# Seven block products in place of eight in the input half of two feed-forward blocks

## The chip, the core and the metric

The kernel runs on one core of a Trainium2 chip. A core has engines that work side by side, each through its own queue of instructions in order: TensorE (PE, with the weight loads shown as PEld), VectorE (DVE), ScalarE (ACT), GpSimd (POOL) and SyncE (SP), which here issues all DMAs. On-chip data lies in SBUF; TensorE writes its results to PSUM[...]. The metric is the device time of one execution in microseconds (us), less is better. "Before" is the median of three runs.

## What is computed

A stack of 128 graphs with 128 nodes of 256 features passes through two layers. Layer 0 is a graph-attention (GAT) layer, layer 1 is a relational multi-head attention with 8 heads and 4 relations. Each ends in a feed-forward block 256 -> 1024 -> 256, and these two blocks are what the change is about.

```python
def _L0_gnn_ref(x, adj, W1, a1, W2, a2, w_ff1, b_ff1, w_ff2, b_ff2, ...):
    h = _gat(x, adj, W1, a1, Fout)
    h = _gat(h, adj, W2, a2, W2.shape[1])
    h = _layernorm(x + h, g_ln1, b_ln1)
    ff = jnp.matmul(jax.nn.relu(jnp.matmul(h, w_ff1) + b_ff1), w_ff2) + b_ff2
    return _layernorm(h + ff, g_ln2, b_ln2)

def _L1_gnn_ref(src, adj_matrix, Wq, bq, Wk, bk, Wv, bv, Wo, bo, W1, b1, W2, b2, ...):
    attn = jax.nn.softmax(jnp.einsum('bhid,bhjd->bhij', q, k) / np.sqrt(dh), axis=-1)
    for r in range(4):
        mask = (adj_matrix == r)[:, None]
        out = out + jnp.einsum('bhij,bhjd->bhid', attn * mask, v_r)
    x = _ln(src + out @ Wo + bo, g1, beta1)
    ff = jax.nn.gelu(x @ W1 + b1, approximate=False) @ W2 + b2
    return _ln(x + ff, g2, beta2)
```

All arithmetic is fp32.

## The kernel before

The 128 graphs are taken in 32 groups of four (G = 4), so a group is T = 512 nodes. Each group goes through five stages, which are Python generators: stage_load (L475), stage_gat (L480), stage_ff0 (L487), stage_attention (L490) and stage_ff1 (L498). A generator emits some instructions and yields a number from the table TIMES (L26), its estimate of how long this step lasts. A heap (L511 to L537) always advances the generator whose virtual time is lowest. A stage of group g starts at 100 g plus the stage's offset (L511) minus an entry of EARLY (L35), so some five groups are in flight, and pieces of different stages alternate in each queue. Within the range KEPT (L36) the order of emission on PE and SP is fixed by added dependencies; on ACT, DVE and POOL a scheduler orders the instructions when the program is built.

The feed-forward block, feed_forward (L256), takes the group's features with the feature index on the partitions (hT, from features, L250). The input half runs over four pairs of 128-row slices of the 1024 hidden units. For each slice two matmuls of 512 columns accumulate the two halves of the 256 input features in one PSUM tile (L266), and ACT reads it once, adds the bias and applies ReLU or GELU into an SBUF tile fT (L269). So there are 16 matmuls and 8 activations per block and group. In block terms, with hidden halves, feature halves and node halves, these are eight products of 512 x 128 x 256 and their sums are formed in PSUM by accumulation. The output half (L278) takes the eight fT tiles as stationary operand: 32 matmuls of 256 columns, whose sum DVE adds to the residual (L279).

All PSUM tiles named mm come from one pool of six; one more bank holds adj, the adjacency of the group as fp32 (L361), and one av, the attention output.

The features are turned by transposed (L224): DVE transposes 32 x 32 blocks into a scratch tile z (one buffer), four DMAs write it to DRAM with the blocks in their new places, and one reads it back (L240 to L245). The exponentials of the attention are turned in place in the same way. In the attention, by_relation (L391) makes for each relation r and half of the heads one masked copy of the turned weights eT on DVE (L397), 128 x 512, eight per graph; the product with the values (L416) reads them. values (L399) computes the values of a graph for the four relations (L404), weights (L364) the scores (L371) and their exponentials (L381).

load_group (L89) fetches three inputs of a group at once: xT for the GAT matmuls, the adjacency mask, and x, which is both the residual and the tile tok in which the group's state lives until it is stored. There are two xT buffers, four for the mask, which is held until the attention has copied it, and six for tok. The first two groups are fetched ahead of most weights (L118 to L128 and L155).

Of the kernel before, what the change touches and what calls it, by code (L numbers as in the profile page):

```python
# [22 lines left out]
P = 128  # L23
# [3 lines left out]
    "ff pair": 5, "ff half": 14.5, "row": 14, "gat": 18, "wh": 6,  # L27
    "gat copy": 3, "qk": 5, "scores": 5, "turn0": 10, "turn1": 5,
    "v0": 3, "mask0": 2, "av": 7, "v": 3, "mask": 3,
    "end": 2, "lead ff0": 30, "lead att": 32, "lead ff1": 31, "affine": 6,  # L30
# [4 lines left out]
EARLY = {(1, 1): 70, (1,2): 50, (2,0): 80, (2,1): 90, (2,2): 90}  # L35
KEPT = {mybir.EngineType.PE: (250, 3150), mybir.EngineType.SP: (0, 4000)}  # L36
# [15 lines left out]
def graph_layers(ctx: ExitStack, tc: tile.TileContext, a: dict, out: bass.AP):  # L52
# [21 lines left out]
    TB, KB = 5, 6  # L74
# [14 lines left out]
    def load_group(g):  # L89
        xt = ld.tile([P, DC, T], F32, name="xt")  # L90
        nc.sync.dma_start(xt, xT[g])
        at = ld.tile([P, G, N], I32, name="at", bufs=4)
        nc.sync.dma_start(at, adjT[g])
        xg = wk.tile([P, G, D], F32, name="tok", bufs=KB)
        nc.sync.dma_start(xg, x[g])
        return xg, xt, at
# [20 lines left out]
    w2T = wload("W2T", wk.tile([P, DC, D], F32, name="w2T", tag="fT", bufs=FC))  # L117
    first_xt = ld.tile([P, DC, T], F32, name="xt")  # L118
    nc.sync.dma_start(first_xt, xT[0])
    w1T = wload("W1T", wk.tile([P, DC, D], F32, name="w1T", tag="fT", bufs=FC))  # L120
    first_at = ld.tile([P, G, N], I32, name="at", bufs=4)
    nc.sync.dma_start(first_at, adjT[0])
    second_xt = ld.tile([P, DC, T], F32, name="xt")
    nc.sync.dma_start(second_xt, xT[1])
    second_at = ld.tile([P, G, N], I32, name="at", bufs=4)
    nc.sync.dma_start(second_at, adjT[1])
    first_x = wk.tile([P, G, D], F32, name="tok", bufs=KB)
    nc.sync.dma_start(first_x, x[0])  # L128
# [26 lines left out]
    second_x = wk.tile([P, G, D], F32, name="tok", bufs=KB)  # L155
    nc.sync.dma_start(second_x, x[1])
# [31 lines left out]

    folded(wf1, bf1, "01")

# [33 lines left out]
    def transposed(y, t, direct, over=False):  # L224
# [14 lines left out]
        z = y if over else wk.tile([P, n, N], F32, name="z", bufs=1)  # L239
# [10 lines left out]
    def features(y, direct):  # L250

        t = t_tile().rearrange("p (b c n) -> p b c n", b=G, c=DC)
        transposed(y.rearrange("p b (c f) -> p (b c) f", f=P), t.rearrange("p b c n -> p (b c) n"), direct)
        return t

    def feed_forward(y, before, direct, win, bin_, wout, func, by=G):  # L256
# [4 lines left out]
        fT = []  # L261
        for f0 in range(0, FC, 2):
            pair = [ps.tile([P, T], F32, name="mm") for _ in range(2)]
            for c in range(DC):
                for i, p in enumerate(pair):
                    nc.tensor.matmul(p, win[:, c, ts(f0 + i, P)], hT[:, :, c], start=c == 0, stop=c == DC - 1)  # L266
            for i, p in enumerate(pair):
                t = wk.tile([P, T], F32, name="fT", tag="fT", bufs=FC)
                nc.scalar.activation(t, p, func, bias=bin_[:, f0 + i:f0 + i + 1])  # L269
                fT.append(t)  # L270
            yield TIMES["ff pair"]
            if f0 in (2, 4):
                affine(y, before, f0 - 2, 2)
        for b2_ in range(0, G, 2):
            p = ps.tile([P, 2, D], F32, name="mm")
            for b in (b2_, b2_ + 1):
                for f in range(FC):
                    nc.tensor.matmul(p[:, b - b2_], fT[f][:, ts(b, N)], wout[:, f], start=f == 0, stop=f == FC - 1)  # L278
# [33 lines left out]
    def gat_block(direct, tag, xg, xt, at):  # L312
# [17 lines left out]
        yield TIMES["gat copy"]  # L330
        att = yield from gat_weighting(wh, D, cap, direct)
        yield TIMES["gat"]
        y = xg
        for b2_ in range(0, G, 2):
# [3 lines left out]
            nc.vector.tensor_add(y[:, b2_:b2_ + 2], xg[:, b2_:b2_ + 2], p)  # L338
        normalised(y)
        return y, at  # L340

    def attention(y, at, first, direct):

        hT = features(y, first or direct)
        yield TIMES["lead att"]
# [40 lines left out]
        def turned(e):  # L386
            eT = wk.tile([P, H, N], F32, name="eT")
            transposed(e, eT, direct, over=True)
            return eT

        def by_relation(b, eT, ms, parts):  # L391


            ab = adj[:, b][:, None, :].to_broadcast([P, HC, N])
            for r, h in parts:
                m = ms[r, h] = wk.tile([P, HC, N], F32, name="m", bufs=DC * R)
                nc.vector.scalar_tensor_tensor(m, ab, r, eT[:, ts(h, HC)], op0=OP.is_equal, op1=OP.mult)  # L397
# [11 lines left out]
        def weighted(ms, v):  # L409
# [3 lines left out]
            for c in range(DC):  # L413
                for r in reversed(range(R)):
                    for q in reversed(range(HC)):
                        last = nc.tensor.matmul(po[ts(q, DH), c], v[:, r, c * P + q * DH:c * P + (q + 1) * DH],  # L416
                                                ms[r, q // 2][:, c * 2 + q % 2],
# [14 lines left out]
        PARTS = [(r, h) for r in range(R) for h in range(2)]  # L432
        v, ms = values(0), {}
        for k in range(0, 8, 2):
            by_relation(0, eT[0], ms, PARTS[k:k + 2])
            yield TIMES["mask0"]
        for b in range(G):
# [8 lines left out]
            for k in range(0, 8, 2):  # L446
                if b + 1 < G:
                    by_relation(b + 1, eT[b + 1], ms, PARTS[k:k + 2])
# [17 lines left out]
    def ff1(y, direct, by):  # L466
        return feed_forward(y, "11", direct, w1, b1, w2, AF.Gelu, by)
# [3 lines left out]
    x0, x1, x2, masks, loads = {}, {}, {}, {}, {}  # L471
    loads[0] = first_x, first_xt, first_at
    loads[1] = second_x, second_xt, second_at

    def stage_load(g):  # L475
        if g > 1:
# [111 lines left out]
```

## Time and profile before

| | before |
|---|---|
| median of 3 runs | 3284.59 us (3283.44 to 3287.23) |
| the profiled execution | 3284.59 us, span of the core 3282.8 us |
| mean granted TensorE clock | 0.989 |
| DMA traffic | 311.11 MB |

Some rows of the costliest groups (line, engine, operation, output <- input with partitions x elements, count, then busy time and mean ns of one, then the idle time just ahead of them and what ended it):

```profile
L397 DVE SCALAR_TENSOR_TENSOR m<-adj,eT 128x512 f32<-128x512 f32 x1024 | 637.2, 680 | 282.1 <-DMA eT<-zd 252.8
L269 ACT ACTIVATE fT<-mm,col 128x512 f32<-128x512 f32 x512 | 333.0, 696 | 392.7 <-PE mm L266 392.3
L266 PE MATMUL mm<-T,w 128*128 128x512 f32 x1024 | 461.1, 598 | 2.3 <-DVE v L405 1.3
L278 PE MATMUL mm<-w,fT 128*128 128x256 f32 x2048 | 454.5, 379 | 0.0
L278 PEld LDWEIGHTS mm<-w,fT 128*128 128x128 f32 x2048 | 388.4, 190 | 80.3 <-issue 31.0
L279 DVE TENSOR_TENSOR tok<-tok,mm 128x512 f32<-128x512 f32 x128 | 88.0, 687 | 421.3 <-PE mm L278 421.2
```

The mean of one PE matmul is not what it costs in a stream, because consecutive matmuls overlap and the ends are modelled; the busy time of the row already takes overlaps within the row out. Every fp32 matmul stands in the trace as two records: L266 issues 512 matmuls for each of the two blocks and has 1024 records.

### The profile page before, as it was taken

The page shows a single profiled execution, that of the slowest core. Times are in us where ns is not written, and L with a number is a line of the kernel's source. Part 1 is how long each engine was busy: PE and PEld are TensorE (multiplying, and loading weights), DVE is VectorE, ACT ScalarE, POOL GpSimd, SP SyncE. Part 2 cuts the span into 40 slices and gives each one's busy share as a digit, 9 for nine tenths or more (in the row PEclk, how much of TensorE's full clock was granted, in tenths as well). Part 3 has the DMA queues.
Part 4 walks back from the last instruction along what each step waited for, and adds up shares of the span by engine and source line. Part 5 has one row for each costly group of instructions (what it writes and reads, how often), then busy time and mean ns, then how long its engine had stood idle before and what let it go on. Part 6 is the DMA issues. An engine that isn't in the chain of part 4 may idle for free.

```text
span 3282.8 us, 50948 instructions
## 1 busy us (share of the span) xinstructions
PE 3217.6 (98%) x18632; PEld 2086.8 (64%) x18632; DVE 1847.3 (56%) x3765; ACT 1531.9 (47%) x4552; POOL 1206.3 (37%) x1480
## 2 busy tenths in 40 slices
PE   6989999999999999999999999999999999999997
PEld 5656666666666666666666666666666666666655
DVE  2375556565555555555555555565565565565552
ACT  3344445545445545445545445545445545445431
POOL 2224334344234344234344234344234344245321
PEclk8999999999999999999999999999999999999998
DMA  5144445344455344454444455344455344454210
GB/s 171 35 111 81 100 110 113 88 98 89 98 112 111 91 97 89 98 112 109 93 92 94 98 112 109 91 97 91 97 113 109 91 100 88 96 113 91 59 33 13
DMA packets 1146571, 311.11 MB, mean 95 GB/s; under 512 B 898256, under 2 KB 1120976, under 8 KB 1146192
## 3 DMA queue, kind: packets, MB, share of 16 engines
q1 hardware_dynamic: 1146320, 307.85, 42.1%
q8 instruction: 147, 2.41, 0.3%
q14 instruction: 104, 0.85, 0.1%
HBM read 178.67 MB, written 129.10 MB: 94 GB/s over the span
## 4 chain that ended last, share of the span: by engine, by line
PE 94%; DVE 3%; DMA 1%; SPq 1%; ACT 1%; POOL 1%; issue 0%; ACTq 0%; DVEq 0%; POOLq 0%
PE mm L278 26%; PE mm L266 26%; PE mm L404 13%; PE av L416 7%; PE mm L371 4%; PE mm L320 3%; PE mm L350 3%; PE mm L356 3%; PE mm L454 3%; PE mm L328 2%; PE mm L337 2%; DVE m L397 1%; SPq L243 1%; DMA zd<-e 1%; DMA eT<-zd 1%; PE mm L184 0%
## 5 line engine op out<-in xcount | busy, mean ns | idle before, releaser
L383 POOL TENSOR_TENSOR e<-e,s 128x512 f32<-128x512 f32 x256 | 277.8, 1091 | 1576.0 <-DVE s L382 1566.8
L397 DVE SCALAR_TENSOR_TENSOR m<-adj,eT 128x512 f32<-128x512 f32 x1024 | 637.2, 680 | 282.1 <-DMA eT<-zd 252.8
L222 POOL TENSOR_TENSOR tok<-tok,ln_rows 128x512 f32<-128x512 f32 (+1 forms) x636 | 659.0, 1055 | 58.2 <-DVE z L240 19.0
L269 ACT ACTIVATE fT<-mm,col 128x512 f32<-128x512 f32 x512 | 333.0, 696 | 392.7 <-PE mm L266 392.3
L404 PE MATMUL mm<-wv,T 128*128 128x512 f32 x1024 | 469.5, 601 | 0.0
L266 PE MATMUL mm<-T,w 128*128 128x512 f32 x1024 | 461.1, 598 | 2.3 <-DVE v L405 1.3
L266 PE MATMUL mm<-T,wf 128*128 128x512 f32 x1024 | 459.3, 597 | 0.0
L278 PE MATMUL mm<-w,fT 128*128 128x256 f32 x2048 | 454.5, 379 | 0.0
L278 PE MATMUL mm<-wf,fT 128*128 128x256 f32 x2048 | 453.4, 379 | 0.0
L278 PEld LDWEIGHTS mm<-w,fT 128*128 128x128 f32 x2048 | 388.4, 190 | 80.3 <-issue 31.0
L381 ACT ACTIVATE e<-mm,nm 128x128 f32<-128x128 f32 x1024 | 359.3, 386 | 160.8 <-DVE nm L377 149.6
L278 PEld LDWEIGHTS mm<-wf,fT 128*128 128x128 f32 x2048 | 388.8, 190 | 67.3 <-issue 15.7
L216 ACT ACTIVATE tok<-tok,nmr,rstd 128x256 f32<-128x256 f32 x512 | 265.8, 591 | 158.5 <-POOL nmr L214 158.4
L404 PEld LDWEIGHTS mm<-wv,T 128*128 128x128 f32 x1024 | 190.4, 191 | 231.6 <-issue 209.1
L266 PEld LDWEIGHTS mm<-T,wf 128*128 128x128 f32 x1024 | 192.7, 191 | 224.1 <-issue 207.9
L266 PEld LDWEIGHTS mm<-T,w 128*128 128x128 f32 x1024 | 192.0, 191 | 218.6 <-issue 207.3
L279 DVE TENSOR_TENSOR tok<-tok,mm 128x512 f32<-128x512 f32 x128 | 88.0, 687 | 421.3 <-PE mm L278 421.2
L416 PE MATMUL av<-m,v 128*32 128x128 f32 x8192 | 255.7, 275 | 8.6 <-DVE v L405 5.0
L359 ACT ACTIVATE kbd<-mm,col 32x512 f32<-32x512 f32 x256 | 173.9, 679 | 191.5 <-PE mm L356 187.4
L416 PEld LDWEIGHTS av<-m,v 128*32 128x32 f32 x8192 | 217.4, 110 | 56.8 <-issue 45.1
L240 DVE STREAM_TRANSPOSE z<-tok 128x1024 f32<-128x1024 f32 x90 | 111.7, 1241 | 242.3 <-ACT tok L216 220.6
L381 ACT ACTIVATION_READ_ACCUMULATOR e<-mm,nm 128x1 f32 x1024 | 231.5, 226 | 0.0
(87 smaller groups left out, 3178.0 us busy)
## 6 DMA issues: line engine op xcount, KB each, us to landing
zd<-e SPq DMA_DIRECT2D x496, 128.0 KB
eT<-zd SPq DMA_DIRECT2D x124, 512.0 KB
zd<-z SPq DMA_DIRECT2D x360, 128.0 KB
T<-zd SPq DMA_DIRECT2D x90, 512.0 KB
xt<-in_xT_dram SPq DMA_DIRECT2D x32, 512.0 KB
tok<-in_x_dram SPq DMA_DIRECT2D x32, 512.0 KB
out_dram<-tok SPq DMA_DIRECT2D x31, 512.0 KB
e<-zsd SPq DMA_DIRECT2D x60, 256.0 KB
```

What stands on the lines that cost most here:

```text
L216: nc.scalar.activation(y[:, b], y[:, b], AF.Identity, bias=nmr[:, b:b + 1], scale=rstd[:, b:b + 1])
L222: engine.tensor_tensor(y[:, b:b + n], y[:, b:b + n], v[:, None, :].to_broadcast([P, n, D]), op)
L266: nc.tensor.matmul(p, win[:, c, ts(f0 + i, P)], hT[:, :, c], start=c == 0, stop=c == DC - 1)
L269: nc.scalar.activation(t, p, func, bias=bin_[:, f0 + i:f0 + i + 1])
L278: nc.tensor.matmul(p[:, b - b2_], fT[f][:, ts(b, N)], wout[:, f], start=f == 0, stop=f == FC - 1)
L359: nc.scalar.activation(kbd[c][rows, :, q % 2], p[rows], AF.Identity, bias=bk[rows, c:c + 1])
L371: nc.tensor.matmul(scores[h][:, c], qT[rows, c, ts(b, N)], kbd[c][rows, b], start=True, stop=True, tile_position=(h * P // 2, 0))
L381: nc.scalar.activation(eh[:, q], p[:, q], AF.Exp, bias=nm[:, q:q + 1], accum_out=s[:, q:q + 1])
L383: nc.gpsimd.tensor_mul(eh, eh, per_row(s, N))
L397: nc.vector.scalar_tensor_tensor(m, ab, r, eT[:, ts(h, HC)], op0=OP.is_equal, op1=OP.mult)
L404: nc.tensor.matmul(p, hT[:, b, f], wv[:, f, r:r + 2], start=f == 0, stop=f == DC - 1)
L416: last = nc.tensor.matmul(po[ts(q, DH), c], v[:, r, c * P + q * DH:c * P + (q + 1) * DH], ms[r, q // 2][:, c * 2 + q % 2], start=r == R - ...
```

## The change

The input half of both blocks is rewritten in Strassen's form (with Winograd's sums). With the weights in four blocks a (feature half by hidden half) and the features in four blocks b (feature half by node half, two graphs each), four sums of the weight blocks are made once (weight_sums, three new tiles, two blocks overwritten) and four sums of the feature blocks are made on POOL for each block and group (moving_sums). Seven products then give all four blocks of the result. A unit computes two slices of each hidden half; in it each product is two matmuls of 256 columns, one for each slice, which fill one PSUM tile. One tile, chain, takes products 1, 6, 7 and 4 in turn, accumulating, and is read by ACT or DVE between them; a second, side, takes 5 and then 3; a third, p, takes 2. ACT copies partial sums to SBUF, DVE adds others onto them, and ACT applies the function at the end: lo in place in SBUF, one half of hi from the chain. Two units run in alternation.

Beside it: masks are made for all heads of a relation at once, 1024 columns; transposed has no tile z of its own any more, features are turned within their target tile; x is fetched only ahead of the second half of the GAT stage, and the mask is fetched a second time for the attention instead of being held; xT has one buffer, the mask two, tok five; the output half takes the hidden slices in the order in which units finish; TIMES, EARLY, the offsets and KEPT have new numbers, and EARLY now has entries for the last groups too.

```diff
 def load_group(g):
-        xt = ld.tile([P, DC, T], F32, name="xt")
+        xt = ld.tile([P, DC, T], F32, name="xt", bufs=1)
         nc.sync.dma_start(xt, xT[g])
-        at = ld.tile([P, G, N], I32, name="at", bufs=4)
+        return xt, load_mask(g)
+    def load_mask(g):
+        at = ld.tile([P, G, N], I32, name="at")
         nc.sync.dma_start(at, adjT[g])
-        xg = wk.tile([P, G, D], F32, name="tok", bufs=KB)
-        nc.sync.dma_start(xg, x[g])
-        return xg, xt, at
+        return at
...
+    def weight_sums(w, name):
+        half = w.shape[-1] // 2
+        a11, a12, a21, a22 = w[:, 0, :half], w[:, 1, :half], w[:, 0, half:], w[:, 1, half:]
+        s1, s2, s4 = (cst.tile([P, half], F32, name=f"{name}s{i}") for i in (1, 2, 4))
+        nc.vector.tensor_add(s1, a21, a22)
+        nc.vector.tensor_sub(s2, s1, a11)
+        nc.vector.tensor_sub(s4, a12, s2)
+        nc.vector.tensor_sub(a21, a11, a21)
+        nc.vector.tensor_scalar(a22, a22, -1.0, None, op0=OP.mult)
+        return None, a11, a12, s4, a22, s1, s2, a21
...
-        z = y if over else wk.tile([P, n, N], F32, name="z", bufs=1)
         nc.vector.transpose(z, y)
...
+    def moving_sums(hT):
+        b11, b21, b12, b22 = (hT[:, h:h + G // 2, c] for h in (0, G // 2) for c in range(DC))
+        t1, t2, t4 = (wk.tile([P, G // 2, N], F32, name=f"t{i}") for i in (1, 2, 4))
+        nc.gpsimd.tensor_sub(t1, b12, b11)
+        nc.gpsimd.tensor_sub(t2, b22, t1)
+        nc.gpsimd.tensor_sub(b12, b22, b12)
+        nc.gpsimd.tensor_sub(t4, t2, b21)
+        return None, b11, b21, b22, t4, t1, t2, b12
...
-        for f0 in range(0, FC, 2):
-            pair = [ps.tile([P, T], F32, name="mm") for _ in range(2)]
-            for c in range(DC):
-                for i, p in enumerate(pair):
-                    nc.tensor.matmul(p, win[:, c, ts(f0 + i, P)], hT[:, :, c], start=c == 0, stop=c == DC - 1)
-            for i, p in enumerate(pair):
-                t = wk.tile([P, T], F32, name="fT", tag="fT", bufs=FC)
-                nc.scalar.activation(t, p, func, bias=bin_[:, f0 + i:f0 + i + 1])
+        hs = moving_sums(hT)
+        def unit(f0):
+            lo, hi = (wk.tile([P, 2, 2, T // 2], F32, name="fT", bufs=FC // 2) for _ in range(2))
...
+            def product(p, k, first=False):
+                for i in range(2):
+                    nc.tensor.matmul(p[:, i], win[k][:, ts(f0 + i, P)], hs[k], start=first and i == 0, stop=True,
+                                     skip_group_check=True)
+            chain, side = (ps.tile([P, 2, T // 2], F32, name="mm") for _ in range(2))
+            product(chain, 1, True)
+            product(side, 5, True)
+            nc.scalar.copy(lo[:, :, 0], chain)
+            nc.scalar.copy(hi[:, :, 1], side)
+            yield
+            p = ps.tile([P, 2, T // 2], F32, name="mm")
+            product(chain, 6)
+            product(p, 2, True)
+            product(side, 3)
+            nc.scalar.copy(lo[:, :, 1], chain)
+            nc.vector.tensor_add(lo[:, :, 0], lo[:, :, 0], p)
+            nc.vector.tensor_add(lo[:, :, 1], lo[:, :, 1], side)
+            yield
+            product(chain, 7)
+            nc.vector.tensor_add(hi[:, :, 1], hi[:, :, 1], chain)
+            yield
+            product(chain, 4)
+            for i in range(2):
+                nc.scalar.activation(lo[:, i], lo[:, i], func, bias=bin_[:, f0 + i:f0 + i + 1])
+            for i in range(2):
+                f = FC // 2 + f0 + i
+                nc.scalar.activation(hi[:, i, 1], hi[:, i, 1], func, bias=bin_[:, f:f + 1])
+                nc.scalar.activation(hi[:, i, 0], chain[:, i], func, bias=bin_[:, f:f + 1])
+            yield
+        units = [unit(0), unit(2)]
+        for n, now in enumerate(((0,), (1,), (0,), (1,), (0,), (1,), (0,), (1,))):
+            for u in now:
+                next(units[u])
...
         yield TIMES["gat copy"]
+        y = wk.tile([P, G, D], F32, name="tok", bufs=KB)
+        nc.sync.dma_start(y, x[g])
...
-                m = ms[r, h] = wk.tile([P, HC, N], F32, name="m", bufs=DC * R)
-                nc.vector.scalar_tensor_tensor(m, ab, r, eT[:, ts(h, HC)], op0=OP.is_equal, op1=OP.mult)
+                m = ms[r] = wk.tile([P, H, N], F32, name="m", bufs=R)
+                nc.vector.scalar_tensor_tensor(m, ab, r, eT, op0=OP.is_equal, op1=OP.mult)
...
-    stages = (stage_load, -81), (stage_gat, -39), (stage_ff0, 50), (stage_attention, 130), (stage_ff1, 298)
+    stages = (stage_load, -81), (stage_gat, -39), (stage_ff0, 48), (stage_attention, 132), (stage_ff1, 300)
```

In the prediction, L numbers are those of the kernel before; L318, where DVE adds a chain after product 7, is the one of the changed kernel, as are "product", "unit" and "chain".

## The prediction

> **What bounds the kernel now.** I read the page from the top, then the windows by stage, then the timeline of one group. First the busy line, the slices and the chain of waits:
>
> ```profile
> PE 3217.6 (98%) x18632; PEld 2086.8 (64%) x18632; DVE 1847.3 (56%) x3765; ACT 1531.9 (47%) x4552; POOL 1206.3 (37%) x1480
> ...
> PE   6989999999999999999999999999999999999997
> ...
> PEclk8999999999999999999999999999999999999998
> ...
> PE 94%; DVE 3%; DMA 1%; SPq 1%; ACT 1%; POOL 1%; issue 0%; ACTq 0%; DVEq 0%; POOLq 0%
> PE mm L278 26%; PE mm L266 26%; PE mm L404 13%; PE av L416 7%; PE mm L371 4%; PE mm L320 3%; PE mm L350 3%; PE mm L356 3%; PE mm L454 3%; PE mm L328 2%; PE mm L337 2%; DVE m L397 1%; SPq L243 1%; DMA zd<-e 1%; DMA eT<-zd 1%; PE mm L184 0%
> ```
>
> TensorE (PE) is busy nearly throughout, at its full clock, and the chain that ended last is PE work for 94%. L266, the half of feed-forward that the change rewrites, is 26% of it. A busy PE can still have gaps, so the windows (columns: PE, PEld, DVE, ACT, POOL busy, clock, DMA share, GB/s):
>
> ```profile
> 164.00:250.00 86.00, 73.01 (x610) 47.85 (x609) 61.96 (x120) 35.49 (x137) 19.53 (x26) 0.96 0.45 106
> 250.00:1200.00 950.00, 948.70 (x5509) 614.27 (x5508) 551.02 (x1117) 459.52 (x1367) 360.44 (x439) 1.00 0.45 98
> 1200.00:2200.00 1000.00, 1000.00 (x5809) 648.59 (x5808) 584.70 (x1192) 485.98 (x1436) 389.30 (x474) 1.00 0.45 100
> 2200.00:3150.00 950.00, 948.84 (x5558) 611.45 (x5557) 547.29 (x1111) 446.24 (x1318) 358.71 (x439) 1.00 0.43 94
> 3150.00:3200.00 50.00, 43.60 (x324) 27.39 (x323) 31.65 (x66) 24.83 (x87) 21.41 (x24) 0.90 0.14 32
> 3200.00:3283.00 83.00, 64.10 (x336) 41.84 (x334) 19.12 (x47) 16.16 (x28) 15.82 (x24) 0.89 0.04 13
> ```
>
> From 250 to 3150 us PE idles 2.5 us in all; its 65 us of idle time (3282.8 - 3217.6) lie at the two ends. So each microsecond of PE work removed in the middle comes off the time, until something else makes PE wait. What a matmul costs is read from the distance between starts, since PE durations overlap. The timeline (start, length, ...):
>
> ```profile
> 1504.72 7.07 PE L278 MATMUL mm<-wf,fT 128*128 128x256 f32 x32
> 1511.62 1.90 PE L328 MATMUL mm<-wh,e 128*128 128x258 f32 x8
> ...
> 1542.02 3.60 PE L266 MATMUL mm<-T,w 128*128 128x512 f32 x8
> 1545.46 1.89 PE L337 MATMUL mm<-wh,e 128*128 128x256 f32 x8
> ```
>
> Each fp32 matmul leaves two records. Four of 512 columns take 1545.46 - 1542.02 = 3.44 us, 0.860 each; sixteen of 256 columns take 6.90 us, 0.431 each. A matmul of half the width costs half, and each with its own weights.
>
> **What the Trainium skill says.** "TensorE: Matmul & The Clock Gate", Part 2, Step-by-step (what each phase is for): a stream of matmuls is paid by its columns, and the next weights load while the current matmul runs. The trace agrees: weight loads take 190 ns inside records spaced 216 ns. "Perfetto Trace Analysis", Tensor Engine Instruction (MATMUL, LD_WEIGHTS): "ACT/DVE/GPSIMD are strict FIFO"; whatever stands behind a waiting instruction waits too. The trace shows it on DVE: L397 idles 252.8 us in 67 waits for eT. The same page, Optimization Strategy: the same gap repeated for a stretch can mean too few buffers for the next tile. No such gap is in the trace before; the new form, which holds PSUM tiles longer, is where one could arise.
>
> **The change, part by part.**
>
> *Products.* Removed: 2 blocks x 32 groups x 16 matmuls x 0.860 = 880.6 us. Added: 64 x 2 units x 7 products x 2 x 0.431 = 772.4 us. PE gains 108.2 us, 3.38 per group. Each of the 28 needs its own weight load, as L278's do, and those run at 0.431.
>
> *Evictions and sums.* ACT lost 16 activations per group at 333.0/512 = 0.650 us (10.4 us), and gets 12 PSUM copies at 0.59 (L237: 575 and 605 ns), 8 activations of 512 at 0.696 and 16 of 256. The last I price from "ScalarE: Activation LUTs", What ACT_TABLE_LOAD costs (280 ns + 0.833 per element with a bias pointer): 493 ns, an estimate; the same formula gives 707 at 512, where the trace has 696. Sum 20.6, so +10.2 us. DVE gets 12 adds at 0.687 (L279), +8.2. The masks go from 32 at 0.680 to 16 of 1024 columns; L455 (256: 410 ns) and L279 (512: 687) give 1.08 ns a column, so 1.24 us each: 21.8 becomes 19.8, -2.0. POOL gets 8 subtractions of 256 at 0.730 (L222's 256 form), +5.8. Per group, from the middle window (a period is 98.5 us, from L266's start at 1501.29 to 1599.79), ACT goes from 48 to 58 us, DVE from 58 to 64, POOL from 38 to 44, in a new period of at least 95.1. None becomes the bound by its sum; PE's 95 us covers them. If that cover fails, it is by order, not by load.
>
> *Order in the middle.* In the order of instructions of the changed kernel I followed one group by hand, with durations of this trace; 0 is the end of the second score pair. PE then has L343's 16 matmuls (6.9), products 1 and 5 of unit 0, the output projection (0.86), 1 and 5 of unit 1, 6, 2, 3 of each unit, 7 of each, two value tiles (3.44), and product 4 of unit 0, wanted at 21.5. Three waits come close:
> (a) Product 4 accumulates on a PSUM tile that DVE (L318) must first read. On DVE four masks stand ahead, which wait for eT. The first e is transposed at about 6.3 (exponentials 1.5, POOL's scaling with the new subtractions between 5.0, transpose 1.25). The way by DRAM and back then took 9.5 us in one case and 13.8 in another (issue of the first write to the first mask):
>
> ```profile
> 1588.95 2.55 SPq L243 DMA_DIRECT2D zd<-e  x4
> ...
> 1598.42 1.29 DVE L397 SCALAR_TENSOR_TENSOR m<-adj,eT 128x512 f32<-128x512 f32 x2 [1.73 <-DMA eT<-zd]
> ...
> 1524.77 6.41 SPq L243 DMA_DIRECT2D zd<-e  x4
> ...
> 1538.54 2.48 DVE L397 SCALAR_TENSOR_TENSOR m<-adj,eT 128x512 f32<-128x512 f32 x4 [6.40 <-DMA eT<-zd]
> ```
>
> With 9.5: masks 15.8 to 20.7, one add, L318 done at 22.1, PE 0.6 late. (b) The next output half (L343) needs a PSUM tile that ACT's exponentials free, behind two normalisations and twelve activations: ready 29.6, wanted 28.9, 0.7 late. (c) In the second block the GAT product (L403) needs a tile freed by DVE behind three masks: ready 9.3, wanted 8.2, 1.1 late. They sum to 2.4 us per group but do not add: a pause of PE moves what PE wants next and leaves ACT and DVE running. My starting times are good to a microsecond at best, so the bounds are 0 and 2.4 per group; I take 0.6, the first wait alone, on 30 groups: +18 us (0 to 72). Queued behind such a PE wait is all of PE; POOL and ACT wait only for products already issued.
>
> *Transposes, loads, ends.* z becomes the target tile itself, which removes a wait of 21.8 us on DVE that PE never felt: 0. Masks are loaded a second time (32 x 256 KB, 8.4 MB on 311) on DMA engines busy 45%: 0 in the middle, in SP's order ahead of an eT return once per group, within the bounds of (a). x comes later, needed only at the second GAT product: 0. At the start the second xt now waits behind all weights: some 11.4 MB at the first windows' 262, 397 and 387 GB/s lands at 32.5 us, its 8 matmuls end at 36, and the product of group 0 behind them began at 37.18 anyway: 0, with up to +6 if the queue holds it. At the end the last blocks have no other group to fill PE, and unit-wise sums leave activations after the last product: +3; the first ones hide theirs partly. Together +2 (-8 to +12).
>
> *Sum.* 3282.8 - 108.2 + 18 + 2 = 3194.6 us of span; 1.8 us lie around it (the profiled execution took 3284.59, which is also the median), so 3196.
>
> **The rivals.**
> Full gain (0.15): no wait of (a) to (c) reaches PE and the ends give 2 us: 3174. For it: PE idles 2.5 us in 2900 today, with DVE waiting for eT all the while. Against: the seven products reuse one tile within 2 to 5 us, where L266 had fresh ones.
> Waits of (a) to (c) all in full (0.19): 3282.8 - 108.2 + 72 + 4 + 1.8 = 3252. For it: the PSUM pool still has six tiles and two units hold four to six of them. Against: a pause forgives the next.
> Slower (0.11), one mechanism: eT's return takes 13.8 us in place of 9.5 at (a). DVE then stands in the masks, the add behind them is 4.9 us late, and PE with it: 30 x 4.9 = 147, so 3282.8 - 108.2 + 147 + 4 + 1.8 = 3327. It decides from a trip of 9.5 + (3.38 - 0.6) = 12.3 us on. For it: the 13.8 above. Against: that trip was slowed by 4 loads and stores just issued on SP; here the order has a transpose's return and a small row ahead.
> The products don't get cheaper (0.03): at 880.6/3584 = 0.246 us per record the gain is gone, 3285. Against it L278's 0.216.
>
> **How the numbers follow.** The forecast (0.52) is 3196, its own range 3178 to 3226 (waits of 0 to 1.6 per group). Two tenths left out below and above: 3168 to 3262 takes in most of the full gain and of the full waits, not the slower case. A measurement can tell about 0.2% (7 us) from no change; faster 0.86 from the first three, same 0.03, slower 0.11.
>
> **What would show it.** The new products spaced 216 ns per record; a period near 95.7 us; PE idle per group under 1.6 us, most of it ahead of product 4 or L343, released by DVE or ACT; ACT near 58 us per group. Wrong if the middle shows PE gaps over 3.4 us a group (the mask wait ahead of L318 would name the slower rival), or if the ends' idle time grows past 77 us.

## The result, and the profile after

The changed kernel takes 3257.3 us (3256.3 to 3257.8), before 3284.3 in the same comparison: ratio 0.9916 [0.9899, 0.9933]. That is 27 us less, not the 88 of the forecast; of the cases listed, the full waits (3252) come closest. The profiled execution's span is 3254.6 us.

The page's busy line and two slice rows of the kernel after:

```profile
PE 3137.8 (96%) x20160; PEld 2371.9 (73%) x20160; DVE 2025.8 (62%) x3647; ACT 1761.5 (54%) x5191; POOL 1379.6 (42%) x1736
...
PE   6989999999999999999999999999999999999988
...
PEclk8999999999999999999999999999999999999999
```

PE is busy 79.8 us less than before (3217.6), but idle for 116.8 us in place of 65.2. The two give the difference of the spans: -79.8 + 51.6 = -28.2. The windows say where the idle time is (columns as before: length, then PE, PEld, DVE, ACT and POOL busy, clock, DMA share, GB/s):

```profile
250.00:1200.00 950.00, 931.07 (x5988) 704.73 (x5987) 606.72 (x1098) 531.23 (x1570) 413.52 (x517) 1.00 0.46 102
1200.00:2200.00 1000.00, 982.34 (x6376) 742.33 (x6376) 644.69 (x1151) 562.19 (x1661) 441.89 (x554) 1.00 0.46 103
2200.00:3100.00 900.00, 885.16 (x5744) 667.92 (x5743) 576.31 (x1040) 495.27 (x1462) 398.08 (x503) 1.00 0.45 100
```

51.4 us of the idle time now lie in the middle, where there were 2.5; at the ends it grew only from 62.7 to 65.4. The chain view of this trace breaks off early (PE has 4% of it), so the waits view of PE, from 250 to 3150 us, has to name the causes (us in total, times, longest; the two other rows of the view are single waits, 6.8 us together):

```profile
PE mm L343 <- ACT e L448: 26.5, 28, 0.9
PE mm L300 <- DVE fT L318: 17.6, 29, 1.0
```

Both come once a group. One group in the timeline of PE (start, length, engine, line, operation; in brackets the idle time before and its releaser):

```profile
1589.40 1.03 PE L300 MATMUL mm<-T,wf 128*128 128x256 f32 x4
1590.27 1.03 PE L300 MATMUL mm<-T,wf1s 128*128 128x256 f32 x4
1591.13 1.89 PE L300 MATMUL mm<-T,wf 128*128 128x256 f32 x8
1592.86 3.60 PE L471 MATMUL mm<-wv,T 128*128 128x512 f32 x8
1597.02 1.96 PE L300 MATMUL mm<-t,wf 128*128 128x256 f32 x8 [0.57 <-DVE fT L318]
1598.92 1.95 PE L483 MATMUL av<-m,v 128*32 128x128 f32 x64
1600.80 1.13 PE L438 MATMUL mm<-kbd,T 64*128 64x256 f32 x8
1601.87 2.47 PE L393 MATMUL mm<-wh,e 128*128 128x258 f32 x8
1605.28 3.07 PE L343 MATMUL mm<-wf,fT 128*128 128x256 f32 x13 [0.94 <-ACT e L448]
```

The third L300 row is the two products 7; the L300 row with the wait holds both products 4. After L393, L343 starts at 1605.28 after another wait, 0.94 for ACT e L448. L343 does not read e; the exponentials read their scores from a PSUM tile of the pool mm, and that tile is what L343 waits for. DVE and ACT in the same stretch:

```profile
1590.47 0.69 DVE L314 TENSOR_TENSOR fT<-fT,mm 128x512 f32<-128x512 f32 x1 [0.25 <-PE mm L300]
1591.07 4.61 DVE L464 SCALAR_TENSOR_TENSOR m<-adj,eT 128x1024 f32<-128x1024 f32 x4
1595.60 0.68 DVE L315 TENSOR_TENSOR fT<-fT,mm 128x512 f32<-128x512 f32 x1
1596.19 1.28 DVE L318 TENSOR_TENSOR fT<-fT,mm 128x512 f32<-128x512 f32 x2
```

```profile
1594.05 4.04 ACT L232 ACTIVATE tok<-tok,nmr,rstd 128x256 f32<-128x256 f32 x8 [3.85 <-POOL nmr L230]
1597.99 1.32 ACT L322 ACTIVATE fT<-fT,col 128x512 f32<-128x512 f32 x2
...
1602.04 1.54 ACT L326 ACTIVATE fT<-mm,col 128x256 f32<-128x256 f32 x4
...
1603.72 0.38 ACT L448 ACTIVATE e<-mm,nm 128x128 f32<-128x128 f32 x1
```

On DVE the four masks stand ahead of the add L318 and keep product 4 waiting. On ACT eight normalisations, themselves waiting for POOL, stand ahead of the twelve activations, and the exponentials that free L343's PSUM tile start only at 1603.72. From 1594.05 until L343 starts ACT has no pause: in this stretch it waits neither for the adds nor for product 4.

From L483's start to the next group's, taken over ten groups, a period is 97.88 us, against 98.50 before. Between starts of matmuls, per group: the input half 27.68 to 24.54 (-3.14); the value products and the wait behind them +0.72; L393 and the wait behind it +1.49; scores +0.20; both output halves +0.12; the rest nothing. The sum is -0.62 before rounding: of 3.14 us gained, 2.52 are given back.

### The profile page after: what moved, and what is told of

It is laid out like the page before. It is cut to its first block, busy times and chain, and to the rows that moved or that the text cites. A ratio compares the mean times of both kernels' runs of the same rounds, so it can differ in the third digit from the quotient of the medians.

```text
span 3254.6 us, 55388 instructions
## 1 busy us (share of the span) xinstructions
PE 3137.8 (96%) x20160; PEld 2371.9 (73%) x20160; DVE 2025.8 (62%) x3647; ACT 1761.5 (54%) x5191; POOL 1379.6 (42%) x1736
## 5 line engine op out<-in xcount | busy, mean ns | idle before, releaser
L464 DVE SCALAR_TENSOR_TENSOR m<-adj,eT 128x1024 f32<-128x1024 f32 x512 | 596.4, 1211 | 170.8 <-DMA eT<-zd 168.3
L238 POOL TENSOR_TENSOR tok<-tok,ln_rows 128x512 f32<-128x512 f32 (+1 forms) x636 | 666.9, 1061 | 70.8 <-ACT tok L232 36.5
L450 POOL TENSOR_TENSOR e<-e,s 128x512 f32<-128x512 f32 x256 | 265.0, 1040 | 524.3 <-DVE s L449 394.1
L343 PE MATMUL mm<-wf,fT 128*128 128x256 f32 x2048 | 456.9, 381 | 26.5 <-ACT e L448 26.5
L343 PE MATMUL mm<-w,fT 128*128 128x256 f32 x2048 | 455.5, 381 | 0.0
L343 PEld LDWEIGHTS mm<-wf,fT 128*128 128x128 f32 x2048 | 387.2, 190 | 91.0 <-ACT e L448 37.8
L448 ACT ACTIVATE e<-mm,nm 128x128 f32<-128x128 f32 x1024 | 360.5, 377 | 167.0 <-DVE nm L444 141.1
L343 PEld LDWEIGHTS mm<-w,fT 128*128 128x128 f32 x2048 | 387.5, 190 | 73.3 <-issue 24.2
L374 POOL TENSOR_TENSOR e<-e,s 128x512 f32<-128x512 f32 x64 | 67.0, 1048 | 492.6 <-DVE s L373 371.9
L483 PE MATMUL av<-m,v 128*32 128x128 f32 x8192 | 255.2, 277 | 17.4 <-DVE m L464 13.3
L483 PEld LDWEIGHTS av<-m,v 128*32 128x32 f32 x8192 | 219.5, 111 | 62.7 <-issue 45.9
L276 POOL TENSOR_TENSOR t<-T 128x256 f32<-128x256 f32 x64 | 46.7, 730 | 499.3 <-DMA T<-zd 498.8
L444 DVE TENSOR_REDUCE nm<-mm 128x4 f32<-128x512 f32 x256 | 163.3, 677 | 125.2 <-PE mm L438 125.2
L448 ACT ACTIVATION_READ_ACCUMULATOR e<-mm,nm 128x1 f32 x1024 | 222.1, 217 | 0.0
L472 DVE TENSOR_TENSOR v<-mm,bv 128x512 f32<-128x512 f32 x256 | 169.5, 683 | 50.4 <-PE mm L471 50.4
L300 PE MATMUL mm<-T,w 128*128 128x256 f32 x768 | 197.3, 387 | 0.2 <-ACT T L253 0.2
L487 ACT COPY oT<-av 128x256 f32<-128x256 f32 x128 | 48.3, 378 | 270.1 <-PE av L483 270.1
```

Source lines behind the costliest of these rows:

```text
L238: engine.tensor_tensor(y[:, b:b + n], y[:, b:b + n], v[:, None, :].to_broadcast([P, n, D]), op)
L300: nc.tensor.matmul(p[:, i], win[k][:, ts(f0 + i, P)], hs[k], start=first and i == 0, stop=True, skip_group_check=True)
L444: nc.vector.tensor_reduce(nm, p, AX.X, OP.max, negate=True)
L448: nc.scalar.activation(eh[:, q], p[:, q], AF.Exp, bias=nm[:, q:q + 1], accum_out=s[:, q:q + 1])
L450: nc.gpsimd.tensor_mul(eh, eh, per_row(s, N))
L464: nc.vector.scalar_tensor_tensor(m, ab, r, eT, op0=OP.is_equal, op1=OP.mult)
```

## The experiments

Ratios and their 95% intervals are against the kernel before. Line numbers move by up to seven where an edit adds lines.

**e1: the old eight products in the changed kernel.** It was to separate the product form from the other edits.

> The changed kernel with the input half put back to eight products as before (two accumulating 512-column matmuls and one activation a slice); everything else as changed: masks of 1024, late x, second mask load, turning in place, new time table. Theory W (the products save 3.14 us of PE a group as they should, and two waits on DVE and ACT, at product 4 and around L393/L343, give 2.15 of it back): with the old input half there is nothing to wait for, PE is full again, a period of 98.5 us, and the time is within 12 us of 3284. Rival S (the edits around the products cost what is missing): 3320 to 3350, with PE idle in the middle.

```diff
-        hs = moving_sums(hT)
...
+            for c in range(DC):
+                for i, p in enumerate(pair):
+                    nc.tensor.matmul(p, win[:, c, ts(f0 + i, P)], hT[:, :, c], start=c == 0, stop=c == DC - 1)
...
+            yield 5
```

Measured: 3535.8, 1.0763 [1.0746, 1.0779]. Both ranges are missed. The run separates nothing, because the new order, made for the new form (TIMES, EARLY, the offsets and KEPT), orders the old one badly: e5 has the same products and side edits, but for the order of slices in the output half, with the old order, and takes 247 us less.

**e2: without the adds.** The twelve adds per group that bring a shared product into its second block (L314, L315, L318) are left out, so the hidden layer lacks those products.

> The changed kernel without the DVE adds of partial sums (L314, L315, L318 left out, so the hidden values are not complete sums and product 4 no longer waits for DVE). PE's work is unchanged. Theory W, waits add: the 0.67 us a group ahead of product 4 goes, 30 groups, 3257 - 20 = 3237 (3228 to 3244). Rival F (a pause forgives the next, one loop of ACT and DVE sets the period, as the prediction assumed): the wait in front of L343 grows by what the other loses, 3252 to 3260.

```diff
-            nc.vector.tensor_add(lo[:, :, 0], lo[:, :, 0], p)
-            nc.vector.tensor_add(lo[:, :, 1], lo[:, :, 1], side)
...
-            nc.vector.tensor_add(hi[:, :, 1], hi[:, :, 1], chain)
```

Measured: 3212.7, 0.978 [0.9763, 0.9796]. The first wait goes. If waits forgave each other, L343's should have grown; it shrank as well (columns as in the waits above):

```profile
PE mm L340 <- ACT e L445: 10.5, 28, 0.4
```

The total gain, 44.6 us, is more than either theory gave. But ACT's order is not the same here: with no adds to wait for, eight of the twelve activations (L319 and L322, 1575.66 to 1579.81 in e2's trace) stand ahead of the normalisations. So the run does not show what a pause at product 4 alone does to L343; e7 does.

**e3 and e4: adj in SBUF, with six and seven PSUM tiles.** Moving adj out of PSUM frees the room of one tile of 128 x 512; e3 moves it alone, e4 also gives the room to the pool "mm". Both have t1, t2 and t4, the sums of the feature blocks, in one buffer each in place of two.

> The changed kernel with adj in SBUF in place of its PSUM bank, still six tiles for matmuls; t1, t2 and t4 single-buffered to make room. It is the control for the next one. W and F both: the same time as the changed kernel, 3250 to 3265, if masks cost the same from SBUF; slower by up to 30 if POOL and DVE hinder each other there.

> As the one before, with the freed bank given to the matmul pool: seven tiles. Theory W says that the 1.48 us a group in L393 and ahead of L343 are waits for a PSUM tile that ACT frees: about 44 us less than the control, near 3213. If the wait is for the activations themselves (fT not ready), or if one loop sets the period (F): within 8 us of the control.

```diff
-        t1, t2, t4 = (wk.tile([P, G // 2, N], F32, name=f"t{i}") for i in (1, 2, 4))
+        t1, t2, t4 = (wk.tile([P, G // 2, N], F32, name=f"t{i}", bufs=1) for i in (1, 2, 4))
...
-        adj = ps.tile([P, G, N], F32, name="adj", bufs=1)
+        adj = wk.tile([P, G, N], F32, name="adj", bufs=1)
...
-    ps = ctx.enter_context(tc.tile_pool(name="ps", bufs=6, space=PSUM))
+    ps = ctx.enter_context(tc.tile_pool(name="ps", bufs=7, space=PSUM))
```

Measured: e3 3396.2 (1.0339 [1.0323, 1.0354]), e4 3347.2 (1.0194 [1.0173, 1.0215]). e3 has the changed kernel's order on every engine and is 139 us slower, for a reason told in the last section. The seventh tile then brings 49 us, and the wait of L343 for ACT e, 24.1 us in e3, is no longer among e4's waits. That fits a wait for a PSUM tile, which is what the place cited in the prediction says of a gap that repeats (the Trainium skill, "Perfetto Trace Analysis", Optimization Strategy: it can mean too few buffers for the next tile). But the scheduler's order on DVE, ACT and POOL in e4 is not that of e3, and its other waits differ from the changed kernel's, so the size of its gain is not that wait's price.

**e5: the side edits alone.** Old order (time table, EARLY, offsets and KEPT), old eight products, with the rest: 1024-column masks, the late x, the second load of masks, transposes in place.

> The kernel before with its own time table and eight products, and only the edits beside the products: masks of 1024, late x, second mask load, turning in the target tile, one xT buffer, two mask buffers, five tok (and one entry of the table, so that group 1 is loaded before it is used). Its order on PE and ACT is nearly that of before, so it separates the edits from the new table, which the first experiment did not. Theory W: the edits are hidden under a full PE: 3276 to 3294. Rival S: over 3300.

```diff
-        hs = moving_sums(hT)
...
+            yield TIMES["ff pair"]
...
-    stages = (stage_load, -81), (stage_gat, -39), (stage_ff0, 48), (stage_attention, 132), (stage_ff1, 300)
+    stages = (stage_load, -81), (stage_gat, -39), (stage_ff0, 50), (stage_attention, 130), (stage_ff1, 298)
```

Measured: 3289.0, 1.0011 [1.0004, 1.0017]. The side edits cost some 4 us (1 to 6 by the interval) where the old order hides them. What was lost comes with the new form and its order.

**e6: the moving sums on DVE; e7: masks of 512 columns in the new order.** Two tests of whether DVE's load delays product 4.

> The changed kernel with the four subtractions of feature blocks on DVE in place of POOL. POOL loses 5.8 us a group, DVE gets 8 adds of 256 columns at 0.41, 3.3 us. If POOL's subtractions, which stand ahead of its scaling of e, make the masks and the normalisation late, the waits at product 4 and L343 shrink: 3225 to 3245. If the length of DVE's queue is what counts, product 4 waits longer: 3262 to 3290. Rival with neither on the path: 3257 within 5.

> The changed kernel with masks of 512 columns again, eight a graph. Each block of masks on DVE gets longer by 8 x 0.68 - 4 x 1.21 = 0.6 us. Theory W (product 4 waits for DVE's add behind a block of masks): the wait of 0.67 us a group grows by about 0.6 unless the scheduler puts the add between masks: 3265 to 3280. Rival (masks not on the path): 3257 within 5.

```diff
-        nc.gpsimd.tensor_sub(t1, b12, b11)
+        nc.vector.tensor_sub(t1, b12, b11)
...
```

```diff
-            ab = adj[:, b][:, None, :].to_broadcast([P, H, N])
+            ab = adj[:, b][:, None, :].to_broadcast([P, HC, N])
...
-                nc.vector.scalar_tensor_tensor(m, ab, r, eT, op0=OP.is_equal, op1=OP.mult)
+                for h in range(2):
+                    nc.vector.scalar_tensor_tensor(m[:, ts(h, HC)], ab, r, eT[:, ts(h, HC)], op0=OP.is_equal, op1=OP.mult)
```

Measured: e6 3283.9 (0.9998 [0.9989, 1.0006]), e7 3261.6 (0.993 [0.9915, 0.9945]). By its time e6 falls into the branch where DVE's length counts, but not by that branch's wait: product 4 waits 18.8 us (17.6 in the changed kernel) and L343 26.6 (26.5); a new 9.0 stands at L393, released by ACT fT L326. More DVE work elsewhere in the period leaves product 4 nearly alone. It costs its 27 us mostly by another way: DVE's L367, ahead of the means and variances from which POOL works out the normalisations, takes 1.71 us a group in place of 1.18. Over twenty groups ACT's normalisations start 12.94 us after product 1 of unit 0 in place of 12.41, L343 starts at 24.18 in place of 23.64, and the period is 98.68 us, 0.80 longer. The rest of the 0.80 I did not resolve. e7's time lies within its rival's range (3257 within 5), but the trace is not the rival's: product 4 waits 26.7 in place of 17.6, as eight short masks last 4.95 us where four long ones last 4.61. Work right ahead of the add counts for product 4, but hardly for the time: product 4 starts 0.22 us later after product 1 of unit 0 (15.68 in place of 15.46), L343 only 0.02 (23.66), and the period is 97.91. ACT's order up to L343's release is the same, so this is what a longer pause at product 4 does by itself: it is taken back ahead of L343.

**e8: normalisations off ACT.** Eight of them, those that stand ahead of the activations, are done on DVE.

> The changed kernel with the scaling of the normalisation after the attention and after the second feed-forward block on DVE (eight operations of 256 columns at about 0.35) in place of ACT (eight at 0.5), so that ACT's activations of the first block have no 4 us of normalisation ahead of them. Theory W: L326, which frees the tiles that L393 needs, and the exponentials behind it come earlier, and the 1.48 us a group at L393 and L343 go for the most part: 3210 to 3235, less what DVE's 2.8 us add to the wait at product 4. Rival (the wait there is the length of the chain itself, not ACT's queue): 3250 or more.

```diff
-            nc.scalar.activation(y[:, b], y[:, b], AF.Identity, bias=nmr[:, b:b + 1], scale=rstd[:, b:b + 1])
+                nc.vector.tensor_scalar(y[:, b], y[:, b], rstd[:, b:b + 1], nmr[:, b:b + 1], op0=OP.mult, op1=OP.add)
```

Measured: 3369.8, 1.0259 [1.0243, 1.0274]. That is within the rival's open range (3250 or more), but not for the rival's reason. The waits of PE in e8:

```profile
PE av L486 <- DVE v L475: 91.7, 28, 3.3
PE mm L303 <- DVE fT L321: 19.0, 29, 1.7
PE mm L346 <- ACT e L451: 11.7, 28, 0.4
```

L343's wait (here L346) falls from 26.5 to 11.7, as the first theory said of a queue on ACT. But DVE got the eight operations between L318 and the second value sum (L475), which they put back by 3.5 us; PE waits 3.3 for it:

```profile
1547.15 1.37 DVE L233 TENSOR_SCALAR tok<-tok,rstd,nmr 128x256 f32<-128x256 f32 x4
1548.44 0.68 DVE L475 TENSOR_TENSOR v<-mm,bv 128x512 f32<-128x512 f32 x1
1549.05 2.32 DVE L233 TENSOR_SCALAR tok<-tok,rstd,nmr 128x256 f32<-128x256 f32 x4
1551.29 0.68 DVE L475 TENSOR_TENSOR v<-mm,bv 128x512 f32<-128x512 f32 x1
```

**e9: the adds first; e10: four ReLUs on POOL; e11: both.** In e9 the first mask of a group is made to stand behind the last L318, by a dependency without a semaphore; PE's order is the same in the middle.

> The changed kernel with one order on DVE turned round, by a dependency without a semaphore: in each group the two adds of L318 stand before the four masks of the same stretch instead of behind them. Same instructions on every engine, same order on PE in the middle. Order theory (product 4 waits because of what stands ahead of its add): the wait of product 4, 17.6 us over 29 groups, goes and nothing takes its place: 3239 (3234 to 3246). Load theory (DVE works without a pause from 1581.8 to 1599.8 in the shown group, so something behind it must be late whatever stands first): the wait moves from product 4 to the value products' consumer L483, released by DVE's masks or value sums; the time stays at 3250 to 3259.

> The changed kernel with four of the twelve activations of the first feed-forward block per group (L325, 256 columns, ReLU) taken from ACT and done by POOL as add and max. ACT theory (L343 waits for a PSUM tile because ACT's exponentials stand behind twelve activations): ACT is 4 x 0.45 = 1.8 us earlier, more than the 0.94 us that L343 waits, so its 26.5 us go, and some of the 18 us of L393's weight load before it: 3220 to 3234. Rival (POOL is the next limit: 4 x 0.73 = 2.9 us are put ahead of the affine steps L238, which then start 2.9 us later, and POOL and DVE hinder each other as with adj in SBUF): 3245 or more, with waits released by POOL tok L238.

> Both edits together. If waits neither forgive nor feed each other, the two single gains add: the changed kernel's 3257 less the gains of the two runs above, 3203 to 3216 by the two first theories, 3220 to 3234 if the order of the adds brings nothing.

```diff
+            later["add"] = nc.cur_bb.bb.instructions[-1].name
...
                 nc.vector.scalar_tensor_tensor(m, ab, r, eT, op0=OP.is_equal, op1=OP.mult)
+                if b == r == 0 and "add" in later:
+                    tc.add_manual_dep(nc.cur_bb.bb.instructions[-1], later["add"], mybir.DependencyInfo(
+                        mybir.DependencyClass.NoSync, mybir.DependencyReason.DATA), reason="adds first")
```

```diff
-                nc.scalar.activation(hi[:, i, 1], hi[:, i, 1], func, bias=bin_[:, f:f + 1])
+                if func == AF.Relu:
+                    nc.gpsimd.tensor_scalar(hi[:, i, 1], hi[:, i, 1], bin_[:, f:f + 1], 0.0, op0=OP.add, op1=OP.max)
+                else:
+                    nc.scalar.activation(hi[:, i, 1], hi[:, i, 1], func, bias=bin_[:, f:f + 1])
```

Measured: e9 3229.4 (0.9836 [0.9823, 0.985]), e10 3216.6 (0.9795 [0.9782, 0.9809]), e11 3252.9 (0.9907 [0.9893, 0.992]). None falls within a stated range: e9 and e10 are faster than theirs, e11 is slower. e9 moves the wait as the load theory said, to L483 (here L487), and 42.4 us are more than product 4's 17.6:

```profile
PE av L487 <- DVE v L476: 42.4, 30, 2.5
```

Yet it gains 28 us: L343's wait is gone. With the adds early, eight of the activations go ahead of the normalisations, in time that ACT had idled (ACT of e9, as above):

```profile
1575.36 1.33 ACT L323 ACTIVATE fT<-fT,col 128x512 f32<-128x512 f32 x2
1578.11 0.91 ACT L326 ACTIVATE fT<-fT,col 128x256 f32<-128x256 f32 x2 [1.42 <-DVE fT L318]
...
1580.94 4.03 ACT L232 ACTIVATE tok<-tok,nmr,rstd 128x256 f32<-128x256 f32 x8
1584.88 1.53 ACT L327 ACTIVATE fT<-mm,col 128x256 f32<-128x256 f32 x4
```

e10 is the reverse: product 4 still waits (18.8), L343 (here L346) no more:

```profile
1583.77 2.01 PE L396 MATMUL mm<-wh,e 128*128 128x258 f32 x8
1585.61 7.07 PE L346 MATMUL mm<-wf,fT 128*128 128x256 f32 x32
```

It gains 41 us, more than its ACT theory's 23 to 37, and is the fastest version with the whole computation, 2.05% below the kernel before. e11 does not add the two. Without the four ReLUs the scheduler orders ACT otherwise, and four normalisations, waiting for POOL, come after the last activations:

```profile
1594.45 1.70 ACT L330 ACTIVATE fT<-mm,col 128x256 f32<-128x256 f32 x4 [1.23 <-PE mm L300]
1597.51 2.08 ACT L232 ACTIVATE tok<-tok,nmr,rstd 128x256 f32<-128x256 f32 x4 [1.36 <-POOL nmr L230]
```

e11 keeps e9's wait at the value sums (40.0) and has 10.5 at L343 again. These do not make up its whole distance from e10; the rest I did not resolve.

**e12: e10 with the GAT masking on POOL.** The one operation of L367 becomes an addition of 0 or -9e15 on POOL, which takes its work off DVE some 8 us ahead of the masks. For it cap, which held 0 or twice BIG, is made to hold 0 or -BIG.

> As the run with the four ReLU activations on POOL (3216.6), and the GAT block's masking of e, the one operation of L367 that takes 0.69 to 1.18 us on DVE in the stretch ahead of product 4, is done by POOL as an addition of 0 or -9e15 instead; by POOL's L374, an operation of the same shape, it costs 1.04 us there, in a gap in which POOL idles 4.3 us. PE's order is the same. Load theory (what is left, about 1 us per group ahead of product 4, is DVE's unbroken queue): DVE reaches L318 0.6 to 1.1 us earlier, and the time falls by 15 to 30: 3187 to 3202. Rival (the add is late for another reason, its products or the masks' eT, or POOL's two-operand work slows DVE): 3212 or more, with the same 18.8 us ahead of product 4 or a new wait released by POOL.

```diff
-        nc.vector.scalar_tensor_tensor(e, cap, BIG, e, op0=OP.subtract, op1=OP.min)
+        nc.gpsimd.tensor_add(e, cap, e)
...
-        nc.vector.tensor_scalar(cap, at, 0, 2 * BIG, op0=OP.is_gt, op1=OP.mult)
+        nc.vector.tensor_scalar(cap, at, 0, -BIG, op0=OP.is_le, op1=OP.mult)
```

Measured: 3232.9, 0.984 [0.9826, 0.9854]. The time is in the rival's range, and the load theory falls: product 4 waits 17.3 us, nearly as before. The rows of PE for product 2 of unit 1 and for product 4, first of e10, then of e12:

```profile
1571.31 1.03 PE L300 MATMUL mm<-T,wf 128*128 128x256 f32 x4
...
1578.93 1.97 PE L300 MATMUL mm<-t,wf 128*128 128x256 f32 x8 [0.57 <-DVE fT L318]
```

```profile
1580.81 1.03 PE L300 MATMUL mm<-T,wf 128*128 128x256 f32 x4
...
1588.43 1.97 PE L300 MATMUL mm<-t,wf 128*128 128x256 f32 x8 [0.56 <-DVE fT L318]
```

Both are 7.62 us apart, and so they are in the changed kernel (1589.40 to 1597.02). DVE falls in step with PE at the second L314, which waits for product 2 (0.25 us in the timeline above). From there it has one add, four masks and two more adds, about 6.5 us to product 4's release, and PE has only 6.0 us of other work. What DVE did earlier did not matter here. e12's 16 us over e10 come with 10.6 us at L343, back again: in ACT's order of e9 and e10 a copy of L393's tile stands ahead of the exponentials, in e2, e11, e12 and the changed kernel it stands behind four of them. The waits fit a part of 0.38 us a group that belongs to that order: it is what L343 still waits in e2, e11 and e12, where ACT idles ahead of these exponentials (0.54 to 1.38 us).

## Why the prediction was wrong

The step that failed is (b), L343's wait for the PSUM tile that ACT frees: "ready 29.6, wanted 28.9, 0.7 late". It is mis-sized, and with it the term "I take 0.6, the first wait alone". On the prediction's clock, where 0 is the end of the second score pair (1574.62 in the group shown), product 4 starts at 22.4, close to the 22.1 worked out, but L343 starts at 30.7. A PE without pauses would want it at about 28.4: its pause ahead of product 4 costs 0.72 us, and from L393's start to L343's it takes 3.41 us where it takes 1.84 in e10, without a wait. So ACT is 2.3 us late in place of 0.7. Per group 0.72 and 1.49 us of it are seen at PE, and with some small terms 2.52 us are given back.

What made the tile late, e6 and e10 show. In e6 one operation on DVE, ahead of what POOL and then ACT need for the normalisations, takes 0.53 us longer; the normalisations start 0.53 us later, L343 0.54 later, and the period grows. In e10 ACT has four activations fewer, L343 starts 1.5 us earlier (a part of it by the order of a copy on ACT: 1.0 in e12), the period is 1.6 us shorter (96.25), and product 4 waits as before. The path is the one through DVE, POOL and ACT: eight normalisations that wait 3.85 us for POOL, then, without a pause, twelve activations and the exponentials. The prediction counted ACT's operations on it, but gave no start for them, so which of its starting times was off stays open.

The reason that it gave for not adding its waits, that a pause of PE "leaves ACT and DVE running", held: in e7 product 4 comes later, L343 does not. By that rule, though, the loss in a stretch is the latest wait and not the first, so its own numbers gave 0.7 here; and (c), in the other block, was left out with nothing worked out that forgives it. That the 2.52 are close to the 2.4 of its three waits is luck: (c), 1.1 of it, did not come, and ACT's lateness was three times its figure. So is the closeness of the full-waits case, 3252.

The adds of L318 bear on ACT in another way, through the order that the scheduler makes. Where they are gone (e2) or come early (e9), eight of the twelve activations stand ahead of the normalisations, in time that ACT had idled, and L343's wait falls to 10.5 us or to nothing.

Point by point:

- Products: right in kind. Their records start 219.1 ns apart on average over the ten groups, 216 typically; 3.14 us per group were gained, not 3.38.
- (a) Product 4 behind L318: right in place and size, 0.6 late forecast, 0.57 idle in the group shown; but by e7 it cost next to nothing, because PE has to wait for ACT afterwards anyway. The cause was half right. The masks do stand ahead of the add, but in the group shown they stand behind the second L314, which waits for PE, and have no wait for eT; the return trip of 13.8 us, and with it the slower rival, did not come at this place.
- (b) L343 behind ACT: right in place and in engine (e10), wrong in size, as told above: 0.94 idle, and about 0.5 more inside L393 (2.47 us in place of 2.01 in e10), whose weight loads wait for ACT fT L326.
- (c) L403 in the second block: 1.1 forecast; no such wait comes once a group.
- Loads: "ACT near 58 us" was about right (562.19 per 1000 us is 55 per period), and no engine's sum became the bound. "If that cover fails, it is by order, not by load" came true in kind.
- Side edits at nothing: e5 gives +4 us. Ends: 2 forecast, 2.7 measured in idle time.
- "Wrong if the middle shows PE gaps over 3.4 us a group": they are 1.8, and the period was still 2.2 us over the forecast 95.7. Some of the loss does not show as a gap, as inside L393, where PE counts as busy.

## What to carry to other kernels

When PE becomes faster in a stretch, list what stands on the other engines between the result PE has just given and the one it needs next, and compare its length with PE's own work in between; load further back did not move product 4's wait here (e6, e12), because DVE waits for PE in that stretch, but it moved L343's, through POOL and ACT (e6). Measure each wait against a PE that has not paused, and take the latest, not the first and not the sum: a pause covers as much of the next wait as it is long (e7). Where a scheduler orders the other engines, read its order again after every edit: e9 and e10, which gained 28 and 41 us, gained 4 together. And look for single operations that can change engine in that stretch: four short activations per group moved to POOL brought 41 us here, the whole change 27.

## What the runs showed of the hardware

Where a mask's operand adj lies changed the time of another engine too. With adj in SBUF in place of PSUM (e3; same instructions, same order on every engine), DVE's masks and POOL's operations both got longer. The single buffers of t1, t2 and t4 are no likely cause: POOL idles 499.4 us ahead of L276, which writes the first of them, and 499.3 in the changed kernel. The groups by shape, of the changed kernel and then of e3 (count, then busy us, mean ns):

```profile
L464 DVE SCALAR_TENSOR_TENSOR m<-adj,eT 128x1024 f32<-128x1024 f32 x512 | 596.4, 1211 | 170.8 <-DMA eT<-zd 168.3 <-PE av L483 1.9 <-DVE s L449 0.3
...
L238 POOL TENSOR_TENSOR tok<-tok,ln_rows 128x256 f32<-128x256 f32 x256 | 188.5, 738 | 7.3 <-DVE mv L224 0.4
```

```profile
L464 DVE SCALAR_TENSOR_TENSOR m<-adj,eT 128x1024 f32<-128x1024 f32 x512 | 674.2, 1362 | 173.8 <-DMA eT<-zd 170.3 <-PE av L483 2.6 <-DVE s L449 0.3
...
L238 POOL TENSOR_TENSOR tok<-tok,ln_rows 128x256 f32<-128x256 f32 x256 | 251.9, 986 | 6.9
```

Masks go from 1211 to 1362 ns on average, POOL's 256-column steps from 738 to 986 ns, and product 4's wait for DVE fT L318 from 17.6 to 64.7 us. It happens only where the two engines work at the same time: in e3 the 303 masks that no tensor operation of POOL overlaps take 1214 ns on average, the 129 that POOL overlaps throughout take 1646, up to 2298. With adj in PSUM the same two kinds take 1211 and 1216 ns. The changed kernel has it as well: DVE's L367, whose operands cap and e both lie in SBUF, takes 0.69 us in the 36 cases without a tensor operation of POOL beside it and 1.19 in the 28 cases with one, once a group, on the path to L343. What couples the two engines no run isolates. Another small surprise: the ReLU of 256 columns takes POOL 1145 ns (e10) where a subtraction of 256 takes 730, and moving it still paid.
